# L1 of a two-layer perceiver: TensorE in source order, keys and values in turn, sums spread by one product

## The chip, the cores and the metric

The kernel runs on one core of a Trainium2 chip. The metric is the time of one execution on the device, in microseconds (us). Before the change three runs gave 3542.09, 3542.24 and 3546.8 us; their median is 3542.24.

The core has engines with a queue each: TensorE (PE: matmuls and transposes), VectorE (DVE), ScalarE (ACT), GpSimd (POOL), and SyncE (SP), which issues nearly all DMAs. They meet through semaphores: an instruction that waits for another engine's result stands at the head of its own engine's queue.

## The reference

A stream `x` of 16 batches x 64 tokens x 512 passes through two layers. Layer 0 (cross attention with a similarity, causal attention, a mixture of experts) isn't touched by the change. Layer 1, in the kernel's terms and shapes:

```
u   = layernorm(x)                                     # 1024 rows: 8 tiles of 128, two batches each
q   = u @ x1_Wq + bq                                   # 16 heads of 32
k   = ctx[b] @ x1_Wk + bk ; v = ctx[b] @ x1_Wv + bv    # 1601 context rows a batch
p   = softmax(mask(q k^T / sqrt(32)))                  # masked keys: no weight
x   = x + (p v) @ x1_Wo + bo                           # cross attention
x   = x + differential_attention_block(layernorm(x))   # within a token, 32 x 32 scores of 16 elements,
                                                       # then a 512-2048-512 ReLU layer
x   = x + ternary_ffn(layernorm(x))                    # 8-bit activations, ternary weights, a
                                                       # 3-tap depthwise convolution, SiLU
```

All is float32 on PE but the ternary products, which are bfloat16.

## The kernel before, in words

`l1_layer` (from L674) walks over steps: one step is one batch `b` and one block `f` of four heads (128 of 512 columns), so 16 x 4 = 64 steps. Two batches share a tile of 128 rows.

A step needs the transposed keys `kT` of its block, 1601 columns in four chunks (`KC`: 384, 384, 384, 449), and the values `v` of the half that its heads lie in (13 blocks of 128 keys, 256 columns). They come from the transposed context, `ctxT`, which is loaded in the same four chunks (`load_ctx`, L751).

- `project_k` (L760) computes one chunk of one block: 4 matmuls into a bank of the pool `ps_mm` (four banks), and ACT moves it out with its bias (L767).
- `project_v` (L770) computes the blocks of one chunk: 4 matmuls of 256 columns into a bank each, and one ACT copy each (L782).
- `scores` (L818) takes two chunks, for the two pairs of heads: four banks, four matmuls over 64 rows (`qbd` holds the queries, block by block), and DVE copies what the mask leaves into the rows `p` (L832), which GpSimd has filled with -1e15 (L1192).
- DVE takes the negated row maximum (L1202), and ACT the exponential with its sum (L1203). This is the softmax of the step; its sums go to `rs8`, 8 columns a batch.
- `transpose_keys` (L171) turns the `p` of the step before, 13 transposes for each of its two halves, into the two banks of `ps_tp`; ACT copies them out as `pT` (L185).
- `attend` (L836) multiplies `pT` with `v`: 52 matmuls of 64 columns by 32, into a bank of `ps_acc` (two banks) that lasts for the batch.
- `finish` (L851), once a batch: a transpose of `rs8`, a reciprocal on 8 partitions (L857), 8 matmuls with the constant `spread` that repeat each head's factor over 32 rows (L861), a copy, and a product with the attention. After an odd batch also the output projection and `residual` (L189: DVE, then GpSimd).

Three generators give work that runs beside the steps: `ternary_weights` during the first pair of batches, `later(t)` (the rest of the layer for tile `t`, from L915, ending in `last`, L1086) during the pair after the tile's own, and `queries` (L785) for the next tile. They stop at each `yield`, and `run` advances them by some stops. `later` has PE work (projections, the hidden layer, ternary products), much DVE work (`products`, L889: 24 pairs of a product L895 and a sum L896), norms (`ln_stats`, `ln_apply`, `norm_T`), and short chains through several engines (`across`, L1070; the transposes of `top` at L1149, of `o` at L992).

What the source names is not the order in which an engine works: a scheduler builds each engine's queue from priorities and modelled times. So the queue of PE before has, for instance, single key matmuls between groups of transposes. Banks of a pool are given out as they come free.

Of the kernel before, what the change touches and what calls it, by code (L numbers as in the profile page):

```python
# [10 lines left out]
F32 = mybir.dt.float32  # L11
# [3 lines left out]
AF = mybir.ActivationFunctionType  # L15
# [4 lines left out]
P = 128  # L20
# [653 lines left out]
def l1_layer(g, d, out):  # L674
# [5 lines left out]
    with ExitStack() as es:  # L680
# [5 lines left out]
        vpool = pool("x1_v", 15)  # L686
# [16 lines left out]
        spread = one.tile([NP, 2, NC, P], F32, tag="spread", name="spread")  # L703
        nc.gpsimd.memset(spread, 0.0)
        for j in range(2):
            for pl in range(2):
                nc.gpsimd.memset(spread[:, j, :, ds((2 * pl + j) * HDX, HDX)], 1.0)
            nc.gpsimd.affine_select(
                out=spread[:, j], in_=spread[:, j], compare_op=ALU.is_equal, fill=0.0,
                base=0, pattern=[[-2, NC], [-1, 2], [0, 2 * HDX]], channel_multiplier=1,  # L710
            )
# [39 lines left out]
        def load_ctx(b):  # L751
            for n, (k0, w) in enumerate(KC):
                tag = "ctxT" if n < 3 else "ctxT_last"
                t = cpool.tile([P, NC, w], F32, tag=tag, name=tag, bufs=None if n < 3 else 1)
                nc.sync.dma_start(
                    out=t, in_=g.ctx_T[b, :, k0 : k0 + w].rearrange("(c p) k -> p c k", p=P)
                )
                ctxs[b, n] = t

        def project_k(b, f, n):  # L760

            w = KC[n][1]
            ps = mm(g)
            mm_k(g, ps[:, :w], lambda c: wk[:, c, ts(f, P)], lambda c: ctxs[b, n][:, c, :])
            tag = "kT" if n < 3 else "kT_last"
            kT = kpool.tile([P, w], F32, tag=tag, name=tag, bufs=None if n < 3 else 2)
            nc.scalar.activation(kT, ps[:, :w], AF.Identity, bias=col(g, "x1_bk", f))  # L767
            kTs[b, f, n] = kT

        def project_v(b, half, n):  # L770

            k0, w = KC[n]
            for k in range((w + P - 1) // P):
                kw = min(P, w - k * P)
                ps = mm(g)
                mm_k(
                    g, ps[:kw, :256],
                    lambda c: ctxs[b, n][:, c, ds(k * P, kw)],
                    lambda c: wv[:, c, ts(half, 256)],
                )  # L780
                v = vpool.tile([P, 256], F32, tag="v", name="v")
                nc.scalar.copy(v[:kw], ps[:kw, :256])  # L782
                vs[b, half, k0 // P + k] = v[:kw]

        def queries(t):  # L785

            u = apool.tile([P, D], F32, tag="u2", name="u")
            ln_apply(g, u, g.x[t], ln_stats(g, small, [g.x[t]]), 0)
            yield
            uT = apool.tile([P, NC, P], F32, tag="u2T", name="uT")  # L790
            nc.scalar.copy(uT, transpose4(g, u))
            yield
            ps = mm(g).rearrange("p (f x) -> p f x", f=NC)
            for f in range(NC):
                if f % 2 == 0:
                    wq = load_cols(d["x1_Wq"], f // 2)
                mm_k(g, ps[:, f, :], lambda c: wq[:, c, ts(f % 2, P)], lambda c: uT[:, c, :])
            qT = spool.tile([P, NC, P], F32, tag="qT", name="qT", bufs=2)
            at, n = _COLS["x1_bq"]
            nc.vector.tensor_tensor(  # L800
                qT, ps, g.cols[:, at : at + n].unsqueeze(2).to_broadcast([P, NC, P]), ALU.add
            )
            qTs[t] = qT
# [47 lines left out]
        def finish(b, po, rs8):  # L851
            t, hb = divmod(b, 2)

            pt = mm(g, tag="tp")
            nc.tensor.transpose(pt[:NP, :P], rs8, g.ident)
            rsT = small.tile([NP, P], F32, tag="rsT", name="rsT")
            nc.vector.reciprocal(rsT, pt[:NP, :P])  # L857
            pr = mm(g, tag="tp")
            for f in range(NC):
                for j in range(2):  # L860
                    nc.tensor.matmul(  # L861
                        pr[:, ts(f, S)], lhsT=spread[:, j, f, :], rhs=rsT[:, ts(j, S)],
                        start=(j == 0), stop=(j == 1),
                    )
            rb = spool.tile([P, NC, S], F32, tag="rb", name="rb")
# [13 lines left out]
            )  # L879
            py = mm(g, tag="acc")  # L880
# [20 lines left out]
        def norm_T(src, gname, bname):  # L901

            z = apool.tile([P, D], F32, tag="z", name="z")
            ln_apply(g, z, src, ln_stats(g, small, [src]), 0)
            yield
# [9 lines left out]
        def later(t):  # L915
# [73 lines left out]

# [14 lines left out]
            for k in range(4):  # L1004
                ps = mm(g).rearrange("p (f x) -> p f x", f=4)
                hid = apool.tile([P, 4, P], F32, tag="hid", name="hid", bufs=2)
                for f in range(4):
                    if f % 2 == 0:
                        w = load_cols(d["W1T"][:, ts(k, 512)], f // 2)
                    mm_k(g, ps[:, f, :], lambda c: w[:, c, ts(f % 2, P)], lambda c: h2T[:, c, :])  # L1010
                    nc.scalar.activation(  # L1011
# [58 lines left out]
        def across(c):  # L1070

            dg = spool.tile([P, P], F32, tag="dg", name="dg")
            nc.vector.tensor_scalar(dg, g.ident, c, None, ALU.mult)
            pb = mm(g, tag="tp")
# [11 lines left out]
        def last(t):  # L1086
# [10 lines left out]
            nc.vector.tensor_scalar(inv, inv, g.tinv[:, 0:1], None, ALU.mult)  # L1097
            yield
# [5 lines left out]
            invb = across(inv)  # L1104
# [3 lines left out]
            for k in range(4):  # L1108
# [4 lines left out]
                yield  # L1113
# [33 lines left out]
            yield  # L1147
            pt = mm(g, tag="tp")
# [4 lines left out]
            nc.vector.tensor_scalar(inv, inv, g.tinv[:, 1:2], None, ALU.mult)  # L1153
            yield
            scb = across(sc)
            qT = apool.tile([P, NF, P], BF16, tag="att", name="qT")
            for k in range(4):
# [4 lines left out]
                if k % 2 == 1:  # L1162
                    yield
            po = mm(g, tag="acc")
# [11 lines left out]


        load_ctx(0)
        for n in range(len(KC)):
            project_k(0, 0, n)  # L1180
            project_v(0, 0, n)
        run(queries(0))
        pending = None
        behind, asked = ternary_weights(), iter(())
        for b in range(B):
            mk, qbd = prepare(b, qTs[b // 2])
            for f in range(NC):
                bk, fk = divmod(b * NC + f + 1, NC)
                ps_ = []
                for j in range(2):  # L1190
                    p = ppool.tile([P, S2], F32, tag="p", name="p")
                    nc.gpsimd.memset(p, -1e15)  # L1192
                    ps_.append(p)
                scores(b, f, (0, 1), ps_, mk, qbd)
                if pending is not None:
                    first = transpose_keys(g, ptpool, pending[2][0], (0, 1), nc.scalar.copy)
                scores(b, f, (2, 3), ps_, mk, qbd)
                if f == 0:
                    sums = small.tile([P, NP], F32, tag="rs8", name="rs8")
                for j, p in enumerate(ps_):  # L1200
                    negm = small.tile([P, 1], F32, tag="negm", name="negm")
                    nc.vector.tensor_reduce(negm, p, AX.X, ALU.max, negate=True)  # L1202
                    nc.scalar.activation(  # L1203
                        p, p, AF.Exp, bias=negm, accum_out=sums[:, 2 * f + j : 2 * f + j + 1]
                    )
                if pending is not None:
                    pTs = [
                        first + transpose_keys(g, ptpool, pending[2][0], (2, 3), nc.scalar.copy),
                        transpose_keys(g, ptpool, pending[2][1], None, nc.scalar.copy),
                    ]  # L1210
                before = pending
                if b % 2 == 1 and f == 0 and b + 1 < B:
                    asked = queries(b // 2 + 1)
                for n in range(len(KC)):
                    if bk < B:
                        project_k(bk, fk, n)
                    if n == 0:
                        if before is not None:
                            attend(*before[:2], pTs, before[3])
                            if f == 0:  # L1220
                                finish(b - 1, *before[3:])
                        if f == 0:
                            po = mm(g, tag="acc")
                            if b % 2 == 0 and b > 0:
                                behind = later(b // 2 - 1)
                        pending = (b, f, ps_, po, sums)
                    if f % 2 == 0 and b + f > 0:
                        project_v(b, f // 2, n)
                    run(behind, 1 if f % 2 == 1 or b % 2 + f == 0 and n < 2 else 3 + f // 2)
                    if n == 3:  # L1230
                        run(asked, 1)
                if f == 2 and b + 1 < B:
                    load_ctx(b + 1)
            if b % 2 == 1:
                run(behind)
        pTs = [transpose_keys(g, ptpool, p) for p in pending[2]]
        attend(*pending[:2], pTs, pending[3])
        finish(B - 1, *pending[3:])
        run(later(NT - 1))


# [121 lines left out]
```

## Time and profile before

| quantity | value |
|---|---|
| median of three runs | 3542.24 us |
| the profiled execution: its time | 3548.19 us |
| its span, first to last instruction | 3546.4 us |
| granted clock of TensorE, mean | 0.968 |
| first scores of L1 | 843.3 us |
| first scores of the last step | 3324.2 us |
| busy: PE, DVE, ACT, POOL | 3275.7, 1652.8, 1140.0, 377.5 us |
| `ps_mm` of values, 256 columns, full chunks | 2304 passes, 523.7 us |
| `ps_mm` of keys, 384 columns | 1536 passes, 555.2 us |
| scores, 384 columns (L824) | 768 passes, 197.7 us |
| transposes of `p` (L182), all layers | 1768 passes, 255.4 us |
| copies under the mask (L832) | 512, 270.4 us |
| row maxima (L1202) | 128, 226.5 us |
| exponentials (L1203) | 128, 208.0 us |

How to read it: a float32 matmul shows as two passes. Ends of matmuls are modelled, so a row's mean is longer than the distance from one start to the next. In the views of waits and of the timeline, a bracket gives the idle time of the engine just before, and whose result ended it; a row with "x8" merges eight neighbours.

### The profile page before, as it was taken

How to read it: one execution, taken by the hardware profiler on the slowest of the kernel's cores; microseconds unless marked ns; L12 is line 12 of the kernel's file. 1: busy time of each engine (PE TensorE's matmuls, PEld its weight loads, DVE VectorE, ACT ScalarE, POOL GpSimd, SP SyncE). 2: the span in 40 equal slices, each digit the busy share in tenths (PEclk: the TensorE clock that was granted, in tenths of full speed). 3: DMA queues.
4: the chain of work that ended last, by engine and by line, in shares of the span. 5: the costliest groups of instructions: out<-in, count | busy, mean ns of one | idle time of the engine just before them, and what ended most of it. 6: DMA issues, size and time to landing. Idle time of an engine off the chain costs nothing. (4 is left out here: it accounts for less than half of the span.)

```text
span 3546.4 us, 49781 instructions
## 1 busy us (share of the span) xinstructions
PE 3275.7 (92%) x21128; PEld 2194.3 (62%) x21128; DVE 1652.8 (47%) x2632; ACT 1140.0 (32%) x2220; POOL 377.5 (11%) x340
## 2 busy tenths in 40 slices
PE   6999999998999999999999999999999999999815
PEld 2444445685677666766767666667667676666514
DVE  2121223116525825653493458256534934581573
ACT  1111021112333434334333434343343334343402
POOL 0000003332101100010001001000100010010000
PEclk9999999999999999999999999999999999999957
DMA  9988413875611133113222321331132123213113
GB/s 361 313 288 304 140 36 107 283 254 174 196 50 50 40 107 103 57 43 123 95 65 74 111 75 40 107 103 57 44 124 97 61 74 111 75 41 107 63 36 122
DMA packets 267374, 418.03 MB, mean 118 GB/s; under 512 B 20736, under 2 KB 164224, under 8 KB 267152
## 3 DMA queue, kind: packets, MB, share of 16 engines
q1 hardware_dynamic: 254656, 370.28, 31.7%
q0 software_dynamic: 12496, 44.57, 3.6%
q8 instruction: 166, 2.72, 0.3%
q14 instruction: 56, 0.46, 0.0%
HBM read 392.26 MB, written 22.54 MB: 117 GB/s over the span
## 5 line engine op out<-in xcount | busy, mean ns | idle before, releaser
L146 PE MATMUL ps_mm<-ctxT,wkv 128*128 128x384 f32 x1536 | 555.2, 492 | 2.0 <-DVE p L832 0.4
L146 PE MATMUL ps_mm<-wkv,ctxT 128*128 128x256 f32 x2304 | 523.7, 380 | 0.0
L146 PEld LDWEIGHTS ps_mm<-wkv,ctxT 128*128 128x128 f32 x2304 | 434.0, 190 | 80.1
L832 DVE COPY_PREDICATED p<-mk,ps_mm 128x384 f32<-128x384 uint8 (+1 forms) x512 | 270.4, 596 | 332.8 <-PE ps_mm L824 332.7
L1192 POOL MEMSET p<- 128x1601 f32 x128 | 185.7, 1453 | 1822.9 <-PE ps_tp L182 1819.1
L146 PEld LDWEIGHTS ps_mm<-ctxT,wkv 128*128 128x128 f32 x1536 | 272.6, 191 | 134.0 <-DVE p L832 7.8
L185 ACT COPY pT<-ps_tp 128x512 f32<-128x512 f32 x504 | 230.7, 504 | 356.2 <-PE ps_tp L182 356.1
L782 ACT COPY v<-ps_mm 128x256 f32<-128x256 f32 (+1 forms) x416 | 152.4, 370 | 417.4 <-PE ps_mm L146 416.7
L182 PEld LDWEIGHTS ps_tp<-ident,p 128*128 128x128 f32 (+1 forms) x1768 | 199.9, 143 | 135.0 <-issue 56.7
L182 PE MATMUL ps_tp<-ident,p 128*128 128x128 f32 (+1 forms) x1768 | 255.4, 282 | 6.4 <-ACT pT L87 3.0
L1202 DVE TENSOR_REDUCE negm<-p 128x1 f32<-128x1601 f32 x128 | 226.5, 1810 | 1.2
L146 PE MATMUL ps_mm<-wkv,ctxT_last 128*128 128x256 f32 (+1 forms) x1024 | 226.2, 379 | 0.0
L895 DVE TENSOR_TENSOR prod<-qkv 128x1024 f32<-128x1024 f32 x128 | 156.5, 1223 | 138.4 <-ACT qkv L927 134.8
L1203 ACT ACTIVATE p<-p,negm 128x1601 f32<-128x1601 f32 x128 | 208.0, 1627 | 15.1 <-DVE negm L1202 14.6
L146 PEld LDWEIGHTS ps_mm<-wkv,ctxT_last 128*128 128x128 f32 (+1 forms) x1024 | 181.1, 177 | 48.6 <-issue 12.1
L146 PE MATMUL ps_mm<-ctxT_last,wkv 128*128 128x449 f32 x512 | 206.4, 540 | 0.0
L824 PE MATMUL ps_mm<-kT,qbd 64*128 64x384 f32 x768 | 197.7, 531 | 8.1 <-DVE qbd L813 8.0
L767 ACT ACTIVATE kT<-ps_mm,cols 128x384 f32<-128x384 f32 x192 | 109.3, 579 | 188.7 <-PE ps_mm L146 188.7
L146 PEld LDWEIGHTS ps_mm<-hT,w 128*128 128x128 f32 x1024 | 132.2, 194 | 56.2 <-ACT hid L1011 40.6
L896 DVE TENSOR_REDUCE att<-prod 128x64 f32<-128x1024 f32 x128 | 155.8, 1217 | 3.7
L146 PEld LDWEIGHTS ps_mm<-ctxT_last,wkv 128*128 128x128 f32 x512 | 95.6, 190 | 81.1 <-issue 73.5
L146 PE MATMUL ps_mm<-hT,w 128*128 128x128 f32 x1024 | 142.6, 283 | 2.4 <-ACT hid L1011 1.0
(291 smaller groups left out, 3872.3 us busy)
## 6 DMA issues: line engine op xcount, KB each, us to landing
ctxT<-in_ctx_T_dram SPq DMA_DIRECT2D x48, 1024.0 KB, 10.4
ck<-in_ctx_dram SPq DMA_DIRECT2D x48, 1024.0 KB, 7.3
ctxT<-in_ctx_T_dram SPq DMA_DIRECT2D x48, 768.0 KB, 4.4
w<-in_W1T_dram SPq DMA_DIRECT2D x64, 512.0 KB, 4.6
w<-in_W2T_dram SPq DMA_DIRECT2D x64, 512.0 KB, 3.7
wt<-tern SPq DMA_DIRECT2D x64, 512.0 KB, 4.2
ctxT_last<-in_ctx_T_dram SPq DMA_DIRECT2D x16, 898.0 KB, 4.8
w<-in_x_Wq_dram SPq DMA_DIRECT2D x16, 512.0 KB, 3.8
```

What stands on the lines that cost most here:

```text
L146: g.nc.tensor.matmul(out, lhsT=lhs(c), rhs=rhs(c), start=(c == 0), stop=(c == n - 1))
L182: g.nc.tensor.transpose(pt[:kw, j, :], p[:, k0 + j * P : k0 + j * P + kw], g.ident)
L185: (out_of or (lambda o, i: evac(g, o, i)))(pT[:kw, :blocks, :], pt[:kw, :blocks, :])
L767: nc.scalar.activation(kT, ps[:, :w], AF.Identity, bias=col(g, "x1_bk", f))
L782: nc.scalar.copy(v[:kw], ps[:kw, :256])
L824: nc.tensor.matmul(bank[:, : KC[n][1]], lhsT=qbd[ts(j, 2 * HDX), f].rearrange("p j s -> p (j s)"), rhs=kTs[b, f, n][ts(j, 2 * HDX), :], st ...
L832: nc.vector.copy_predicated(ps_[j][:, k0 : k0 + w], mk[:, k0 : k0 + w], bank[:, :w])
L895: nc.vector.tensor_tensor(pr, qv.unsqueeze(2).to_broadcast([P, CH, 32, 16]), kv, ALU.mult)
L896: nc.vector.tensor_reduce(out[:, ts(i, CH * 32)], pr.rearrange("p i j d -> p (i j) d"), AX.X, ALU.add)
L1192: nc.gpsimd.memset(p, -1e15)
L1202: nc.vector.tensor_reduce(negm, p, AX.X, ALU.max, negate=True)
L1203: nc.scalar.activation(p, p, AF.Exp, bias=negm, accum_out=sums[:, 2 * f + j : 2 * f + j + 1])
```

## The change

- PE's queue is no longer scheduled: `tc.manual_schedule` around all of L1 puts PE's instructions in the order of the source. The other engines are scheduled as before.
- The loop over steps becomes a function `step` that names its work in a fixed order: first scores, transposes, a unit of projection, transposes, a stop of `later` (`slot`), and so on.
- Before, each step computed the keys for the next step, and even steps also half the values. Now odd steps compute keys, of two blocks at once (`project_k(b, h)`), and even steps values (`project_v(b, half)`).
- Values are computed two blocks to a bank, with one copy for both; the pool of values has 10 tiles of two blocks in place of 15 of one.
- `spread` and the transpose of `rs8` go. `widen` builds on DVE, from the reciprocals and a constant `side`, a matrix with each head's factor in its 32 columns, and one matmul a block with `fold` (two identities of 64, one above the other) gives the factors.
- Chains get more stops, so that a transpose comes one stop later than what it needs (two `yield` before it); `across` is cut in two (`diagonal` on DVE, then the matmul); the four ReLUs follow all 16 matmuls of their block; the stop between a ternary product and its scaling goes.

```diff
-        def project_k(b, f, n):
...
+        def project_k(b, h):
+
+            for n, (_, w) in enumerate(KC):
+                for f in (2 * h, 2 * h + 1):
+                    ps = mm(g)
+                    mm_k(g, ps[:, :w], lambda c: wk[:, c, ts(f, P)], lambda c: ctxs[b, n][:, c, :])
...
+                    yield
+        def project_v(b, half):
+
+            for k in range(0, len(KT), 2):
+                ps = mm(g).rearrange("p (j n) -> p j n", j=2)
+                v = vpool.tile([P, 2, 256], F32, tag="v", name="v")
...
+                nc.scalar.copy(v[:kw, : len(blocks)], ps[:kw, : len(blocks)])
+                yield
+        def widen(rs8):
...
+            nc.vector.reciprocal(r8, rs8)
+            wide = spool.tile([P, NP, 2, HDX], F32, tag="wide", name="wide")
+            nc.vector.tensor_tensor(
+                wide, r8.unsqueeze(2).unsqueeze(3).to_broadcast([P, NP, 2, HDX]),
+                side.unsqueeze(1).unsqueeze(3).to_broadcast([P, NP, 2, HDX]), ALU.mult,
+            )
-        def finish(b, po, rs8):
+        def finish(b, po, wide):
...
-            pt = mm(g, tag="tp")
-            nc.tensor.transpose(pt[:NP, :P], rs8, g.ident)
-            rsT = small.tile([NP, P], F32, tag="rsT", name="rsT")
-            nc.vector.reciprocal(rsT, pt[:NP, :P])
             pr = mm(g, tag="tp")
             for f in range(NC):
-                for j in range(2):
-                    nc.tensor.matmul(
-                        pr[:, ts(f, S)], lhsT=spread[:, j, f, :], rhs=rsT[:, ts(j, S)],
-                        start=(j == 0), stop=(j == 1),
-                    )
+                nc.tensor.matmul(
+                    pr[:, ts(f, S)],
+                    lhsT=wide[:, ts(f, 2)].rearrange("p h j d -> p (h j d)"), rhs=fold,
+                    start=True, stop=True,
+                )
...
+        def step(b, f, before, mk, qbd):
...
+            def slot():
+                if resting == 0:
+                    run(behind, 1)
+            resting = b % 2 + f == 0
...
+            if f % 2 == 0:
+                work = project_v(b, f // 2) if b + f > 0 else iter(())
+            else:
+                bk, h = (b, 1) if f == 1 else (b + 1, 0)
+                work = project_k(bk, h) if bk < B else iter(())
+            unit = 2 - f % 2
+            scores(b, f, (0, 1), ps_, mk, qbd)
+            if f == 0 and before is not None:
+                wide = widen(sums[b - 1])
+            turn(0, (0, 1))
+            run(work, unit)
+            turn(0, (2, 3))
+            slot()
+            turn(1, (0,))
+            scores(b, f, (2, 3), ps_, mk, qbd)
+            for j, p in enumerate(ps_):
+                negm = small.tile([P, 1], F32, tag="negm", name="negm")
+                nc.vector.tensor_reduce(negm, p, AX.X, ALU.max, negate=True)
+                nc.scalar.activation(
+                    p, p, AF.Exp, bias=negm, accum_out=sums[b][:, 2 * f + j : 2 * f + j + 1]
+                )
+            turn(1, (1,))
+            run(work, unit)
+            turn(1, (2, 3))
+            slot()
+            run(work, unit)
+            ending = iter(())
+            if before is not None:
+                attend(*before[:2], pTs, pos[before[0]])
+                if f == 0:
+                    ending = finish(b - 1, pos.pop(b - 1), wide)
+                    run(ending, 1)
+            slot()
+            run(work, unit)
+            run(ending)
...
+            resting = 0
+            run(asked, 1)
+            slot()
+            for _ in range(5 - f % 2):
+                run(work, 1)
+                slot()
+            run(asked, 1)
+            run(work)
+            slot()
+            if f == 2 and b + 1 < B:
+                for n in range(len(KC)):
+                    load_ctx(b + 1, n)
...
-        load_ctx(0)
-        for n in range(len(KC)):
-            project_k(0, 0, n)
-            project_v(0, 0, n)
-        run(queries(0))
...
+        with tc.manual_schedule(engines={mybir.EngineType.PE}):
+            for n in range(len(KC)):
+                load_ctx(0, n)
+            run(project_k(0, 0))
+            run(project_v(0, 0))
+            run(queries(0))
```

Here `turn(j, ns)` transposes chunks `ns` of half `j` of the step before.

## Prediction

> **What bounds the kernel now.** I read the busy shares first, then the granted clock, then one stretch of the second layer (which I call L1), then who waits for whom there, and last single steps.
>
> ```profile
> PE 3275.7 (92%) x21128; PEld 2194.3 (62%) x21128; DVE 1652.8 (47%) x2632; ACT 1140.0 (32%) x2220; POOL 377.5 (11%) x340
> ...
> PE   6999999998999999999999999999999999999815
> ...
> PEclk9999999999999999999999999999999999999957
> ```
>
> TensorE (PE) is the bound from the tenth slice to the 37th. L1 repeats with a period of two batches, because one tile of 128 rows holds two: the even batch's first scores start at 1078.1, 1403.7, 1728.2, 2053.0, 2379.1, 2702.4 and 3028.5 us in the timeline, on average 325.1 apart. I name the eight steps of such a pair e0 to e3 and o0 to o3 (even or odd batch, f = 0 to 3). The windows view of one pair (busy us and count of PE, PEld, DVE, ACT and POOL, then clock and DMA):
>
> ```profile
> 2379.00:2702.40 323.40, 312.76 (x2252) 222.66 (x2251) 175.19 (x260) 129.18 (x252) 29.52 (x22) 1.00 0.26 82
> ```
>
> PE stands still for 10.6 of 323 us here. The waits of PE over the six pairs from 1078 to 3028 us say for whom:
>
> ```profile
> PE ps_acc L842 <- ACT pT L185: 24.2, 36, 1.3
> PE ps_mm L824 <- DVE p L832: 21.7, 23, 2.0
> PE ps_tp L1149 <- ACT pT L185: 7.4, 6, 1.2
> PE ps_mm L146 <- ACT oT L992: 4.0, 6, 0.7
> PE ps_mm L146 <- ACT uT L1103: 2.7, 6, 0.4
> ```
>
> They sum to 60.0 us, 10.0 a pair. A matmul's modelled end runs about 0.16 us past the next start (14 key passes of 0.323 are 4.52 us, shown as 4.68), so 77 waits hide another 2 us a pair: 12.0. That is all that a better order of PE can win; the rest is matmuls that stay.
>
> **The change part by part.**
>
> *Matmuls.* Keys, values, scores, attention and the later layers issue the same passes (a float32 matmul has two), so their sum stays; two value blocks in a bank only halve ACT's copies, which lie beside PE. *Sums:* now 16 passes take 1.93 us (963.50 to 965.43) plus a transpose of 0.11. Four matmuls in place of eight halve the passes: 0.96. Gain 1.07 a batch, 2.1 a pair; the new `wide` on DVE (one 512-wide operation, 0.69 like L877, plus a small reciprocal, against a reciprocal of 0.95) is issued some 12 us before it is used.
>
> *Waits removed:* at most the 12.0. Together 14.1 a pair.
>
> *Waits added.* In the built program PE follows the source, so nothing can be slipped in front of a late instruction, and everything behind it waits too. [...] If later matmuls could pass, the list below would be nothing and L1 would gain 14 a pair; by the rule each wait counts in full. The trace sides with the rule: the last L1149 idles PE 5.20 us at 3337 with an attend queued behind. I therefore follow chains through ACT's and DVE's built order.
>
> (1) *Step o3, the transpose of `top`.* In the built order ACT does, after the second score group, two copies, table load, exp, key copy, exp and only then the two `pT` copies; `top` needs the bank of the first. The same chain today, o3 at 2678, on PE and then on ACT:
>
> ```profile
> 2682.40 0.77 PE L182 MATMUL ps_tp<-ident,p 128*128 128x128 f32 x5
> ...
> 2685.86 4.68 PE L146 MATMUL ps_mm<-ctxT,wkv 128*128 128x384 f32 x14
> 2691.77 0.33 PE L1149 MATMUL ps_tp<-ident,top 128*128 128x128 f32 x1 [1.23 <-ACT pT L185]
> ```
>
> ```profile
> 2686.62 1.28 ACT L1203 ACT_TABLE_LOAD   x1 [1.11 <-DVE negm L1202]
> 2687.91 1.63 ACT L1203 ACTIVATE p<-p,negm 128x1601 f32<-128x1601 f32 x1
> ...
> 2689.54 1.61 ACT L1203 ACTIVATE p<-p,negm 128x1601 f32<-128x1601 f32 x1
> ...
> 2691.15 0.72 ACT L185 COPY pT<-ps_tp 128x512 f32<-128x512 f32 x2
> ```
>
> From the end of the scores (2682.40) to `top` it takes 9.4 us, and PE covers all but 1.23. After the change only 4 transposes (0.44), one key chunk (8 passes, 2.58) and 5 transposes (0.55) stand there, 3.6 us, as PE's built order shows (a `Matmult` is two passes, a transpose one; K is a key chunk):
>
> ```
> scores x4 | ident,p x4 | K | ident,p x4, x1 | ident,top | K | attend | K | dg,ones ...
> ```
>
> The wait is 5.8.
>
> [...] The row says 1.28, and exp follows 0.01 later. [...] I take the row.
>
> (2) *Attend behind both exps.* Scores to attend, by rows: copies end 1.65 us after the scores (four in 2.13, starting 1.0 after the group's start), maximum 1.77, exp 1.63 and again 1.63 with gaps of 0.1, a value or key copy 0.55, `pT` copies 0.75: 8.3, and 1.28 more with a table load (waits of this kind, 0.67 us on average, are the first row of the list above). PE's cover in a value step is 0.44+3.45+0.55+3.45 = 7.9. So e0 waits 0.4, o0 about 1.5, o2 about 2.0 (DVE's convolution sits between). e2 and e3 come out at 1.9 each, DVE being late. Sum 7.7.
>
> (3) *DVE late in e1 to e3.* Attention products of the later layer are 2 x 1.255 us a unit. A copy behind them in DVE's order waits:
>
> ```profile
> 2781.27 1.22 DVE L895 TENSOR_TENSOR prod<-qkv 128x1024 f32<-128x1024 f32 x1
> 2782.53 1.22 DVE L896 TENSOR_REDUCE att<-prod 128x64 f32<-128x1024 f32 x1
> 2783.78 1.22 DVE L895 TENSOR_TENSOR prod<-qkv 128x1024 f32<-128x1024 f32 x1
> 2784.92 0.58 DVE L832 COPY_PREDICATED p<-mk,ps_mm 128x384 f32<-128x384 uint8 x1
> ```
>
> Today six units run at the end of e0. After the change one and a half do, and 22.5 fall into e1 to e3: 56.5 us, with copies and maxima (3 x 7.75) and the softmax and scaling (about 14) 94 us, against PE work of 89.5. In the built order two product units stand between the two score groups' copies, so the banks come late. From e1's start, in us: its first copies (0.5 each, a 1.25 reduction between) end at 4.5, two units at 9.5, the next copy at 10.1, where PE stands ready at 8.7: 1.4. Seven units then hold DVE until 35.3; e2 starts at 31.3, wants its bank at 33.7 and has it at 35.9: 2.25. Its second group finds DVE busy from 38.7 to 45.0, bank at 45.65 against 43.15: 2.5. e3 the same way 0.85 and 2.5. Sum 9.5.
>
> (4) *Third transpose bank.* The source now has 4+1 transposes, then 4 more into the first bank, with ACT's key or value copy (0.55) ahead of the bank's own (0.50): freed 1.3 after the chunk, wanted at 0.55. That is 0.75 in the six steps whose slot there holds no PE work (o1 and o2 have some): 4.5.
>
> (5) *Normalization.* In e0 the transpose of `z` stands three value blocks (5.2 us) behind the output projection; the chain (residual, GpSimd, two norms) took 6.8 in the tail (3361.28 to 3368.04) and has a second norm interleaved here: 8.5, a wait of 3.3. In o0 the hidden layer follows its transposes at once, with four ACT rows of 0.38 each: 1.3. Sum 4.6.
>
> Together 32.1 a pair. Hand-followed chains overstate: a late PE lets the others catch up. The ends are 0 (all covered) and 32.1; I take three quarters, 24, since (1), the largest single wait, rests on a measured chain. Net 24 - 14.1 = +10 a pair, seven pairs +70.
>
> *The front.* PE waits 4.0 for `u` at 823 and 8.0 for `qbd` at 835. Ten more us of keys cover the first; DVE's reductions, which delayed `qbd`, now come earlier. But the second step's transposes follow two score groups with nothing between: some 6 us for maximum, table and exp. Net -5. Pair 0 (no later layers): waits of kinds 2 and 4, some 16, and DVE's weight rounding, some 5, against 235 measured less 223 of work: +10. The tail keeps its DVE chain (73.6 us of PE idle for L988); the last step, without key work, orders `top` before the final transposes: +3.
>
> *DMAs.* Context chunks keep bytes and place (after f = 2), and the built SP order puts weights in between, as before: 4.4 us to land, needed 20 later: nothing. Uncovered, a chunk costs up to 4.4 a batch.
>
> Sum: the profiled run took 3548.2, its span 3546.4; +70 - 5 + 10 + 3 = +78 gives 3624 of span. The median of the runs is 3542.2, so **3620**.
>
> **The rivals.** *Half the waits* (16 a pair): +2 x 7 + 8 = +22, 3564. For it: many of the waits are differences near 1 us. Against: (1). *Faster:* the cover holds. It decides at new waits of 13 a pair; with only (1) and half of (4), 8, L1 gains 6 a pair: 3542 - 43 + 8 = 3507; with none 3542 - 99 + 8 = 3451. For it: copies of scores now have a key or value chunk between the groups, where today 8 transposes (1.0 us) meet four copies (2.1). Against: the order of the exps before the copies, in six of eight steps. *DVE as the bound:* all 32.1 and more, some 35 a pair: +21 x 7 + 8 = 3697; for it 94 against 89.5, against it DVE's 175 us in a pair of 323. *The change does nothing:* the built order moves as the source says, so this is only a draw of gains and losses.
>
> **How the numbers follow.** Likeliest case (3585 to 3685) 0.50, half the waits (3550 to 3585) 0.20, faster 0.20, a draw 0.04, DVE-bound 0.06. 0.2% (7 us) is about what a measurement tells from no change. Range 3500 to 3685: it leaves out the DVE case and the better half of the faster one. Faster 0.20, same 0.04, slower 0.76.
>
> **What would show it.** Right: waits of PE for `pT` at `top` near 6 us in each o3, waits for `p` copies in e1 to e3, a pair period near 335, PE's idle time up from 10 to some 25 a pair, fewer passes under the sums. Wrong: a period under 325, or `top` and attend without waits, which would mean that ACT's order or PE's cover isn't as I read it.

## The result, and the profile after

The changed kernel takes 3590.82 us (median of 4 runs, 3588.24 to 3591.26) where the kernel before takes 3542.16 in the same series: 1.0133 times as long, 95% interval 1.0115 to 1.0150. The prediction was 3620, slower. The profiled execution has 3591.18 us and a span of 3589.4, 43.0 more than before.

Busy shares and slices, from the page of the changed kernel:

```profile
PE 3219.8 (90%) x20976; PEld 2161.4 (60%) x20984; DVE 1627.0 (45%) x2649; ACT 1097.0 (31%) x2028; POOL 372.0 (10%) x336
...
PE   6999999998999899999999998999899999989815
...
PEclk9999999999999999999999999999999999999957
```

PE is busy for 56 us less and the kernel takes 43 us more. Several slices of L1 that stood at 9 now stand at 8.

The pairs of batches start at 1091.6, 1425.2, 1757.6, 2088.7, 2419.6, 2753.1 and 3085.4 us: six periods of 332.3 on average, against 325.05. One of them in the windows view of the changed kernel (columns as before):

```profile
2419.60:2753.10 333.50, 310.16 (x2235) 221.49 (x2235) 172.35 (x262) 123.80 (x228) 29.21 (x22) 0.98 0.25 80
```

PE stands still for 23.3 us where it was 10.6. For whom, the waits of PE over these six pairs tell (line waited at, releaser: us in total, times, longest):

```profile
PE ps_acc L847 <- ACT pT L185: 35.4, 24, 1.8
PE ps_mm L146 <- DVE p L837: 33.3, 30, 1.9
PE ps_tp L1170 <- ACT pT L185: 32.8, 6, 5.5
PE ps_tp L182 <- ACT pT L185: 21.9, 36, 0.6
PE ps_tp L126 <- DVE z L117: 13.1, 6, 2.2
PE ps_mm L146 <- ACT hT L924: 3.6, 6, 0.6
```

Together 140.1 us, 23.35 a pair (before 10.0). L847 is attend, L146 after `p` a key or value chunk that wants a bank of scores, L1170 `top`, L182 the keys' transposes, L126 `z`.

The largest single one, step o3 of the fifth pair, from the timelines of PE and then of ACT:

```profile
2718.21 0.81 PE L829 MATMUL ps_mm<-kT,qbd 64*128 64x384 f32 x4
2718.95 0.66 PE L182 MATMUL ps_tp<-ident,p 128*128 128x128 f32 x4
2719.45 2.75 PE L146 MATMUL ps_mm<-ctxT,wkv 128*128 128x384 f32 x8
...
2722.03 0.71 PE L182 MATMUL ps_tp<-ident,p 128*128 128x128 f32 x5
...
2728.20 0.47 PE L1170 MATMUL ps_tp<-ident,top 128*128 128x128 f32 x1 [5.46 <-ACT pT L185]
2728.47 5.33 PE L146 MATMUL ps_mm<-ctxT,wkv 128*128 128x384 f32 x8
```

```profile
2722.58 1.28 ACT L1248 ACT_TABLE_LOAD   x1 [2.35 <-DVE negm L1247]
2723.88 1.63 ACT L1248 ACTIVATE p<-p,negm 128x1601 f32<-128x1601 f32 x1
...
2725.51 1.61 ACT L1248 ACTIVATE p<-p,negm 128x1601 f32<-128x1601 f32 x1
...
2727.12 0.56 ACT L765 ACTIVATE kT<-ps_mm,cols 128x384 f32<-128x384 f32 x1
2727.58 0.73 ACT L185 COPY pT<-ps_tp 128x512 f32<-128x512 f32 x2
```

`top` has been ready long before; what it lacks is a bank of the transposes, and the copy that empties it stands on ACT behind a table load, two exps and a key copy. The key chunk behind `top` needs none of that and waits with it. Its eight passes then take 5.33 us, where the chunk ahead took 2.75: this comes back below.

### The profile page after: what moved, and what is told of

It reads as the page before. It is cut to its first block, busy times and chain, and to the rows that moved or that the text cites. A ratio compares the mean times of both kernels' runs of the same rounds, so it can differ in the third digit from the quotient of the medians.

```text
span 3589.4 us, 49320 instructions
## 1 busy us (share of the span) xinstructions
PE 3219.8 (90%) x20976; PEld 2161.4 (60%) x20984; DVE 1627.0 (45%) x2649; ACT 1097.0 (31%) x2028; POOL 372.0 (10%) x336
## 4 chain that ended last, share of the span: by engine, by line
PE 63%; DVE 24%; ACT 6%; DMA 4%; issue 2%; POOL 1%; SPq 1%; ACTq 0%; POOLq 0%; DVEq 0%
PE ps_mm L146 37%; PE ps_acc L146 7%; DVE prod L909 6%; DVE att L910 4%; DVE p L837 4%; PE ps_mm L829 3%; DVE negm L1247 3%; PE ps_acc L1034 3%; PE ps_tp L182 3%; PE ps_mm L240 2%; ACT p L1248 2%; PE ps_acc L847 2%; PE ps_acc L274 2%; DVE o L910 2%; DMA ck<-in_ctx_dram 2%
## 5 line engine op out<-in xcount | busy, mean ns | idle before, releaser
L146 PE MATMUL ps_mm<-ctxT,wkv 128*128 128x384 f32 x1536 | 538.4, 499 | 23.8 <-DVE p L837 23.8
L146 PE MATMUL ps_mm<-wkv,ctxT 128*128 128x256 f32 x2304 | 523.9, 381 | 18.9 <-DVE p L837 18.9
L146 PEld LDWEIGHTS ps_mm<-wkv,ctxT 128*128 128x128 f32 x2304 | 427.4, 190 | 76.3 <-DVE p L837 22.5
L146 PEld LDWEIGHTS ps_mm<-ctxT,wkv 128*128 128x128 f32 x1536 | 288.3, 195 | 209.5 <-DVE p L837 29.0
L182 PE MATMUL ps_tp<-ident,p 128*128 128x128 f32 (+1 forms) x1768 | 260.6, 280 | 39.2 <-ACT pT L185 30.3
L182 PEld LDWEIGHTS ps_tp<-ident,p 128*128 128x128 f32 (+1 forms) x1768 | 199.1, 141 | 157.1 <-issue 74.0
L146 PE MATMUL ps_mm<-wkv,ctxT_last 128*128 128x256 f32 (+1 forms) x1024 | 236.6, 386 | 0.0
L786 ACT COPY v<-ps_mm 128x512 f32<-128x512 f32 (+1 forms) x224 | 122.4, 549 | 314.8 <-PE ps_mm L146 314.0
L146 PEld LDWEIGHTS ps_mm<-wkv,ctxT_last 128*128 128x128 f32 (+1 forms) x1024 | 182.7, 180 | 37.5
L146 PE MATMUL ps_mm<-ctxT_last,wkv 128*128 128x449 f32 x512 | 199.4, 539 | 0.0
L829 PE MATMUL ps_mm<-kT,qbd 64*128 64x384 f32 x768 | 164.0, 509 | 4.1 <-DVE qbd L818 4.1
L146 PEld LDWEIGHTS ps_mm<-ctxT_last,wkv 128*128 128x128 f32 x512 | 97.1, 190 | 91.3 <-issue 82.0
L847 PE MATMUL ps_acc<-pT,v 128*32 128x64 f32 (+1 forms) x6656 | 106.5, 220 | 47.7 <-ACT pT L185 47.3
L847 PEld LDWEIGHTS ps_acc<-pT,v 128*32 128x32 f32 (+1 forms) x6656 | 96.2, 110 | 78.5 <-ACT pT L185 65.3
## 6 DMA issues: line engine op xcount, KB each, us to landing
ctxT<-in_ctx_T_dram SPq DMA_DIRECT2D x48, 1024.0 KB, 10.6
```

Of the source, the lines that this page charges most:

```text
L146: g.nc.tensor.matmul(out, lhsT=lhs(c), rhs=rhs(c), start=(c == 0), stop=(c == n - 1))
L182: g.nc.tensor.transpose(pt[:kw, j, :], p[:, k0 + j * P : k0 + j * P + kw], g.ident)
L786: nc.scalar.copy(v[:kw, : len(blocks)], ps[:kw, : len(blocks)])
L829: nc.tensor.matmul(bank[:, : KC[n][1]], lhsT=qbd[ts(j, 2 * HDX), f].rearrange("p j s -> p (j s)"), rhs=kTs[b, f, n][ts(j, 2 * HDX), :], st ...
L847: nc.tensor.matmul(po[ts(r, HDX), ts(f, S)], lhsT=vs[b, f // 2, k][:, ts(4 * (f % 2) + r, HDX)], rhs=pTs[r // 2][k][:, ts(r % 2, S)], star ...
```

## The experiments

All twelve runs (median; ratio to the kernel before with 95% interval; mean period of six pairs; waits of PE that the profile lists, a pair):

| kernel | us | ratio | pair | waits |
|---|---|---|---|---|
| before | 3542 to 3544 | 1 | 325.05 | 10.0 |
| changed | 3590.8 | 1.0133 [1.0115, 1.0150] | 332.3 | 23.35 |
| e_sched | 3486.8 | 0.9845 [0.9829, 0.9862] | 317.65 | 7.0 |
| e_bman | 3857.6 | 1.0890 [1.0871, 1.0908] | 365.5 | 37.9 |
| e_fold | 3526.8 | 0.9950 [0.9933, 0.9967] | 323.3 | 10.1 |
| e_exps | 3553.9 | 1.0031 [1.0021, 1.0042] | 327.7 | 17.2 |
| e_top | 3566.2 | 1.0062 [1.0045, 1.0079] | 328.1 | 21.0 |
| e_half | 3539.4 | 0.9989 [0.9982, 0.9996] | 329.8 | 19.5 |
| e_tpz | 3587.5 | 1.0129 [1.0112, 1.0146] | 331.5 | 19.85 |
| e_tp | 3554.0 | 1.0032 [1.0020, 1.0043] | 327.35 | 17.7 |
| e_four | 3504.0 | 0.9893 [0.9874, 0.9912] | 320.15 | 12.4 |
| e_five2 | 3502.1 | 0.9878 [0.9861, 0.9894] | 320.0 | 11.9 |
| e_mends | 3471.8 | 0.9795 [0.9779, 0.9812] | 315.8 | 9.2 |
| e_best1 | 3481.4 | 0.9828 [0.9802, 0.9855] | 318.5 | 6.8 |

### The three parts of the change, apart

**e_sched**: all but the order.

```
-        with tc.manual_schedule(engines={mybir.EngineType.PE}):
+        if True:
```

> The changed kernel with PE's order left to the planner again; the repacked keys and values, the new place of each piece and the sums by an identity stay. Theory (the order is what costs): PE's waits fall from 23 to near 12 us a pair, and with 2 us of sums saved the kernel comes out at or a little under the kernel before, 3520 to 3550. Rival (repacking costs): it stays near 3590.

3486.8: better than either theory, 56 us under the kernel before and 104 under the changed one. The repacking is no cost but a gain, and the order alone costs 14.65 us a pair net (the order also wins something, in the scores; that is counted below). Waits of PE over six pairs:

```profile
PE ps_mm L146 <- DVE p L837: 22.1, 12, 2.3
PE ps_acc L847 <- ACT pT L185: 14.9, 18, 1.6
PE ps_tp L126 <- DVE z L117: 2.7, 6, 0.5
PE ps_mm L829 <- ACT v L786: 1.2, 6, 0.2
PE ps_mm L146 <- ACT hT L924: 1.0, 6, 0.2
```

No line for `top` and none for the transposes' third bank (L182). The timeline of PE in o3 shows what the planner did, from the second transposes on:

```profile
2646.66 2.75 PE L146 MATMUL ps_mm<-ctxT,wkv 128*128 128x384 f32 x8
...
2649.24 0.71 PE L182 MATMUL ps_tp<-ident,p 128*128 128x128 f32 x5
...
2649.78 5.33 PE L146 MATMUL ps_mm<-ctxT,wkv 128*128 128x384 f32 x16
...
2654.95 0.27 PE L1170 MATMUL ps_tp<-ident,top 128*128 128x128 f32 x1
2655.15 1.66 PE L847 MATMUL ps_acc<-pT,v 65*32 65x64 f32 x104
```

ACT's order is as late as in the changed kernel, but two more key chunks (16 passes, 5.33 us at a granted clock of 1.00) are slipped in front of `top`, and it finds its bank free. That is what a fixed order takes away.

**e_bman**: the order alone. The L1 loop of the kernel before, unchanged, is put under the same line that fixes PE's order.

```
+        with tc.manual_schedule(engines={mybir.EngineType.PE}):
             load_ctx(0)
             for n in range(len(KC)):
                 project_k(0, 0, n)
...
```

> The kernel before with one part of the change alone: PE follows the order of its source, nothing else is touched. There the second scores follow four score matmuls and eight transposes, and attend follows all transposes and one key chunk. Theory (a fixed order turns short cover into waits): the second scores wait about 2 us and attend 4 to 5 us in each of eight steps, besides the chains of the later layers; a pair grows by 30 to 50 us and the kernel to 3780 to 3900. So the change's new places for the work earn most of that back. Rival (the order of PE costs little by itself, the repacking does): within 20 us of 3542.

3857.6, within the range: +40 a pair. So the new places of the work, with the repacking, earn back most of what the fixed order costs in the old ones (the sums are 1.8 of these 33 us a pair, see e_fold); the first line of its waits is attend's, 92.3 us in 36 waits of up to 3.8.

**e_fold**: the sums alone. `widen`, `fold` and the four matmuls of the changed `finish` are put into the kernel before.

```
-            pt = mm(g, tag="tp")
-            nc.tensor.transpose(pt[:NP, :P], rs8, g.ident)
...
-                for j in range(2):
-                    nc.tensor.matmul(
-                        pr[:, ts(f, S)], lhsT=spread[:, j, f, :], rhs=rsT[:, ts(j, S)],
...
+                nc.tensor.matmul(
+                    pr[:, ts(f, S)],
+                    lhsT=wide[:, ts(f, 2)].rearrange("p h j d -> p (h j d)"), rhs=fold,
```

> The kernel before with the sums by an identity alone: widen on DVE, four matmuls in place of a transpose and eight, nothing else. Theory: 1.07 us less PE work in each of 16 batches, 17 us: 3525. Rival (PE stands idle elsewhere by what is saved, or the planner moves other work for the worse): no change, 3540 to 3550.

Minus 16.8 us, 1.05 a batch. This term of the prediction (1.07) is settled.

### What PE waits for in the fixed order

**e_exps**: PE's order untouched, one exp later on ACT.

```
             scores(b, f, (2, 3), ps_, mk, qbd)
-            for j, p in enumerate(ps_):
-                negm = small.tile([P, 1], F32, tag="negm", name="negm")
-                nc.vector.tensor_reduce(negm, p, AX.X, ALU.max, negate=True)
-                nc.scalar.activation(
-                    p, p, AF.Exp, bias=negm, accum_out=sums[b][:, 2 * f + j : 2 * f + j + 1]
-                )
             turn(1, (1,))
             run(work, unit)
             turn(1, (2, 3))
+            for j, p in enumerate(ps_):
...
             slot()
```

> One edit to the changed kernel: a step's maxima and exps are named after the last transposes of the keys instead of ahead of them. PE's order is the same; on ACT the second exp then stands behind the last two pT copies, where it stood ahead of them. Theory (PE in a fixed order waits for pT copies that stand behind exps of 1.63 us on ACT): attend's waits, 5.9 us a pair, mostly vanish, top's 5.5 falls to about 3.9, a pair is shorter by 5 to 7.5, the kernel by 35 to 55 us: 3535 to 3555. Rival (the repacked keys and values, or DVE, set the pace, and ACT's order only decides where the wait is shown): the waits move to the copies of the scores and the time stays within 10 us of 3591.

3553.9, 37 us less than the changed kernel, within the theory's 35 to 55; a pair wins 4.6, a little less than the 5 to 7.5 expected. Of its waits:

```profile
PE ps_mm L146 <- DVE p L837: 33.0, 24, 3.1
PE ps_tp L1170 <- ACT pT L185: 23.1, 6, 3.9
...
PE ps_acc L847 <- ACT pT L185: 1.3, 6, 0.2
```

Attend's 35.4 us shrink to 1.3 and `top`'s 5.5 to 3.9: one exp (1.63) off the chain. Waits for copies of scores stay at 33, and a new kind appears, 7.5 us for copies of values (not shown).

**e_top**: one more place for `top`.

```
             yield
             yield
+            yield
             pt = mm(g, tag="tp")
             nc.tensor.transpose(pt[:, :P], top, g.ident)
```

> The changed kernel with the transpose of top named one place later: behind attend of step o3 instead of ahead of the key chunk before attend. Theory (both wait for the same pT copies, which come late on ACT): top's 5.5 us go, but attend, at 2.6 us of key chunk behind the transposes, now waits about 3.5, so a pair wins 2 and the kernel 14: 3570 to 3580. Rival (the place of top is the cause by itself): all 5.5 are won in seven pairs, 38 us: 3552.

3566.2: 25 us less, between the two. As the theory says, attend takes over (first line below, now with six more waits of 3.0); the listed waits fall by 2.4 a pair, but the period falls by 4.2, as PE's busy time falls by 1.8 too (308.9 to 307.1), though the matmuls are the same.

```profile
PE ps_acc L847 <- ACT pT L185: 53.7, 30, 3.0
PE ps_mm L146 <- DVE p L837: 33.4, 30, 1.9
```

The clock accounts for this: over the six pairs its records show 51.2 us at half rate in the changed kernel (granted clock 0.98 in three pairs, 0.99 in three) and 23.9 in e_top (0.99 in all six). Windows of o3 in the changed kernel: the chunk ahead of `top`, the one behind it, and the next (the third number from the end is the granted clock):

```profile
2719.50:2722.00 2.50, 2.50 (x10) 1.42 (x9) 2.50 (x5) 0.58 (x1) 0.00 (x0) 1.00 0.05 10
2728.50:2733.70 5.20, 5.20 (x9) 2.33 (x8) 1.23 (x7) 0.00 (x0) 0.00 (x0) 0.50 0.02 3
2735.40:2738.00 2.60, 2.60 (x16) 1.63 (x9) 0.00 (x0) 0.00 (x0) 0.00 (x0) 1.00 0.03 6
```

Behind these 5.46 us without work PE's granted clock is 0.50; eight passes take 5.33 us where the chunk ahead took 2.75. From the start of this chunk to the start of what follows, the half clock adds 1.5 to 2.6 us in each of the six pairs, 1.9 on average. So the wait at `top` costs 5.5 and about 1.9 on top of it.

**e_half**: half of the later layers' products on DVE are left out.

```
+            nc.gpsimd.memset(out, 0.0)
             for i in range(n // CH):
+                if i % 2 == 1:
+                    yield
+                    continue
```

> The changed kernel with every second unit of attention products of the later layers left out (zeros in their place); their slots stay empty. Theory (products on DVE hold up copies of scores in e1 to e3): waits for p copies, 5.6 us a pair, fall below 1, attend's in e2 and e3 fall with them, a pair goes from 332.3 to 324 to 327; outside the pairs the tail, where PE stands idle for these products, is shorter by about 30. Together 3505 to 3530. Rival (DVE has time enough and the fixed order of PE alone makes the waits): a pair stays within 2 of 332 and only the tail is shorter, 3555 to 3565.

Between the two: the tail is 30 us shorter as both said, but a pair only 2.5. Waits for `p` copies fall from 33.3 to 16.9, attend's only from 35.4 to 28.6: those of e2 and o0 are gone, but e3's rises from 1.7 to 2.9.

```profile
2172.18 5.28 PE L146 MATMUL ps_mm<-wkv,ctxT 128*128 128x256 f32 x16 [2.21 <-DVE p L837]
...
2220.92 1.66 PE L847 MATMUL ps_acc<-pT,v 65*32 65x64 f32 x104 [2.94 <-ACT pT L185]
```

DVE's load is a part of the loss, the smaller one. The first line also shows a wait of 2.21 and behind it 16 value passes in 5.28 us, where the 16 in the next place, at 2181.53, take 3.72.

**e_tpz** and **e_tp**: the third transpose bank, with `z` one place later and without.

```
-            turn(1, (0,))
             scores(b, f, (2, 3), ps_, mk, qbd)
...
-            turn(1, (1,))
+            turn(1, (0, 1))
```

and, in e_tpz alone, in `norm_T`:

```
             ln_apply(g, z, src, ln_stats(g, small, [src]), 0)
             yield
             yield
+            yield
             pt = transpose4(g, z)
```

> The changed kernel with two of the five pieces alone: the second keys' first transposes behind the second scores instead of ahead of them, and z's transpose one place later. Theory: the waits for the third transpose bank, 3.65 us a pair, go, but where attend waits after them (four of the six steps) it takes a part over; z's 2.2 falls to 0.5; a pair wins 3 to 4.5, the kernel 20 to 32: 3559 to 3571. Rival (attend's chain swallows all of the bank's waits): only z's 1.7 a pair are won, 12 us: 3579. Rival on the other side (waits add up freely): 5.3 a pair, 37 us: 3554.

> The changed kernel with the second keys' first transposes behind the second scores instead of ahead of them, and nothing else. Both moves of the run before together won 3 us; there z's later place also pushed each later piece by one, and a new wait of 4.1 us for pT copies stood at the first transposes of the ternary layers. Theory (the bank's wait is a real loss of its own where nothing late follows it in the step): e0 and e1 win 0.6 each, and in the steps that wait for exps the second scores start 0.44 earlier and the chain to attend with them: 2 to 3.5 a pair, 14 to 25 us: 3566 to 3577. Rival (the waits at attend and top take all of it over): within 7 us of 3590.

e_tpz misses: 3587.5, hardly anything won. e_tp, which was run to find out why, wins 37 us, more than either side expected. Waits of e_tp and then of e_tpz:

```profile
PE ps_acc L847 <- ACT pT L185: 44.8, 24, 4.3
PE ps_tp L1170 <- ACT pT L185: 30.2, 6, 5.0
PE ps_mm L146 <- DVE p L837: 14.7, 17, 1.9
```

```profile
PE ps_acc L847 <- ACT pT L185: 71.0, 30, 4.3
PE ps_tq L1123 <- ACT pT L185: 24.4, 6, 4.1
```

In both the line of L182 (21.9) is gone. In e_tp waits for copies of scores fall as well, from 33.3 to 14.7, which I hadn't counted; attend rises by 9.4, since in e1 the planner of ACT now puts a table load and both exps ahead of the last `pT` copy. The one `yield` more at `z` pushes every later piece by one place, and the first transposes of the ternary layers (L1123) come to stand where `top` stood: 4.1 us each, and attend 26.2 more than in e_tp. So a place that looks good for one piece cost 33 us through the pieces behind it.

### The same order, named better

**e_mends**: five pieces moved, PE still in the named order (the edits of e_exps, e_tp, e_top and `z` as shown, and the slots of the even batch):

```
             turn(0, (2, 3))
-            slot()
+            if b % 2 == 1:
+                slot()
...
             run(work)
             slot()
+            if b % 2 == 0:
+                slot()
```

> The changed kernel, still with PE in the named order, with five pieces named elsewhere: exps behind the last pT copies; the transposes of the second keys behind the second scores instead of one ahead of them; top one place later; the transpose of z one place later; in the even batch the later layers' first slot of a step at its end. Theory (the loss is where things are named, not that an order is fixed): the five kinds of wait fall from 23 to some 6 us a pair, a pair is near 316, the kernel 3465 to 3495, as with the planner's order. Rival (a fixed order can't follow the other engines, the waits move on): a pair stays above 325 and the kernel above 3540.

3471.8, 119 us less than the changed kernel and 72 less than before. Its waits (first two lines):

```profile
PE ps_mm L146 <- DVE p L837: 34.5, 17, 2.8
PE ps_acc L847 <- ACT pT L185: 8.3, 12, 1.0
```

What remains is DVE: 5.75 a pair for copies of scores, no less than in the changed kernel.

**e_four** takes the slots' move out again, **e_five2** puts the moved slot behind the maxima instead of at the step's end.

```
             turn(1, (2, 3))
...
             slot()
+            if b % 2 == 0:
+                slot()
```

> The five pieces less one: exps, the second keys' transposes, top and z as before, but the later layers' slots of the even batch where the change has them. Theory (products stand ahead of copies at the one end of a step or at the other, DVE is short of time in e1 to e3 either way): within 10 us of 3472. Rival (a slot between two score groups is what holds the copies up): the copies' waits rise again and the kernel to 3485 or more.

> The five pieces, with the even batch's first slot of a step moved only behind the maxima (two units in one place) instead of to the step's end. Theory (copies of the next step's first scores then meet a shorter row of products): waits for p copies fall from 5.75 to about 3 us a pair, a pair of 313, the kernel 3450 to 3462. Rival (the products of e1 to e3 fill DVE to the step's end anyway): within 5 us of 3472.

Both are 30 us slower than e_mends and like each other (3504.0, 3502.1). For e_four the rival's time holds but not its reason, since waits for copies of scores rise by only 4.4 us over six pairs; for e_five2 neither holds. Waits of e_four:

```profile
PE ps_mm L146 <- DVE p L837: 38.9, 21, 3.1
PE ps_tq L1123 <- ACT pT L185: 14.8, 6, 2.5
PE ps_acc L847 <- ACT pT L185: 13.3, 12, 1.6
```

In e_mends the slot at the end of e0 is one more than before (the first slot of e0 rests), so its later pieces stand one place earlier; in these two they don't, and the ternary transposes wait 2.5 in place of 0.6. I read the 30 us as the shift again, now undone; no run has the extra slot alone, so how much of it is DVE's order stays open.

**e_best1**: e_sched with e_exps' edit.

> The changed kernel with PE left to the planner and exps named behind the last pT copies. Theory: attend's remaining waits, 2.5 us a pair with the planner's order alone, go; a pair of 315 to 316, 3470 to 3482. Rival (PE then waits for the copies of the scores instead, DVE's products being in front of them): no change from the planner's order alone, 3487 within 5.

3481.4, which lies in the theory's range. But its runs spread from 3474 to 3494, so the 5 us to e_sched are not clear of noise. Attend's waits do go (14.9 to 1.6 us over six pairs), but new ones for the copies of scores and of values take their place, and the profiled pairs are no shorter (318.5, before 317.65): in mechanism the rival is nearer. The named order of e_mends is at 0.9795 and this at 0.9828; their intervals overlap. That of e_sched, 0.9845, does not overlap with e_mends: a well-named fixed order beat the planner's own by 15 us.

## Why the prediction was right, and where it wasn't

**Direction and mechanism.** PE follows the source, what is late holds up all behind it, and waits of PE rose by 13.35 us a pair. e_sched and e_bman show the order as the cause, e_exps that ACT's exps stand in the chain. Of the 78 us that the prediction added to the kernel, 49 came.

**The waits, term by term** (predicted, then measured a pair): (1) `top` 5.8, 5.5. (2) Attend 7.7, 5.9. (3) DVE late 9.5, 5.55. (4) The third bank 4.5, 3.65. (5) `z` and hidden layer 4.6, 2.8. Sum 32.1, measured 23.35; "I take three quarters, 24" was right, but the factor was set between 0 and 32.1 without a measurement: that it came out at 0.73 is in part luck. The largest error is (3): followed by hand, e2 alone was to lose 4.75 and lost 2.4 (0.90 and 1.49 in the fourth pair), I think because PE came later to each bank by the waits before it; no run shows that apart.

**The table load.** The row's 1.28 us held: after the change too the load takes 1.28, and exp follows 0.02 after its end (2722.58 to 2723.88). Between load and exp, where more would have lengthened the chain, nothing else shows.

**What a pair loses net: +10 predicted, +7.25 measured.** The step that failed is "issue the same passes, so their sum stays", and with it "12.0 a pair. That is all that a better order of PE can win; the rest is matmuls that stay". From 23.35 of waits to +7.25 something must have brought 16.1, not 14.1, although the half clock took some 2.9 of it back (1.9 behind `top`, 1.0 behind `z`): in all 19. The listed waits of before are 10.0 of this, and e_fold gives 1.8 to the sums. The largest part of the rest is in the scores: the same passes take less time. One group of second scores, in step e1, before and then in the changed kernel, each up to the row that follows it:

```profile
2441.30 1.10 PE L824 MATMUL ps_mm<-kT_last,qbd 64*128 64x449 f32 x3 [0.70 <-DVE p L832]
...
2443.53 0.66 PE L182 MATMUL ps_tp<-ident,p 128*128 128x128 f32 x4
```

```profile
2477.20 1.02 PE L829 MATMUL ps_mm<-kT_last,qbd 64*128 64x449 f32 x4
2478.06 0.81 PE L829 MATMUL ps_mm<-kT,qbd 64*128 64x384 f32 x4
2478.80 0.66 PE L182 MATMUL ps_tp<-ident,p 128*128 128x128 f32 x4
```

Eight passes take 2.23 us there and 1.60 here. A score matmul is 64*128 in its row, where a key pass is 128*128. In the changed kernel the eight passes start in four pairs, two neighbours 0.006 to 0.007 us apart; in the group of before the first and the last start alone, 0.46 and 0.43 from their neighbours, and the six between in pairs 0.02 to 0.04 apart. The changed kernel's second scores take 1.60 in all 48 steps of the six pairs, before 2.16 on average (half clock in five of six e3 is a part of that). Together both groups of a pair's eight steps fall from 31.7 us, 0.4 of them listed waits, to 26.1, which is 5.2 more than the lists show; some 2.0 are spread over other rows. This gain needs the fixed order and the new places: in the planner's order the same scores take 32.3 (e_sched), 33.4 (e_best1) and 31.8 (e_fold), in a fixed order with the old places 29.6 (e_bman), and 26.4 in e_mends, which is why e_mends can be faster than e_sched with more waits in its list. In e_sched the planner puts transposes between two score matmuls. Before, that banks come singly from DVE is my reading of the first row's wait; no run tests it. The prediction had 2.0 us for such hidden time.

**The last pair: the largest miss.** The spans' difference of 43.0 splits, by the starts of the pairs, into the front -0.8 (the first scores of L1 start at 842.5 us, before at 843.3; predicted -5), pair 0 +14.3 (+10), six pairs +43.4 (+60), and the last pair with the tail -13.9, where I had +13. "Seven pairs +70" counted the last like the others. But its o3 has no keys to compute, and after the change that is two blocks instead of one: a block is 24 passes of 0.323 and 8 of 0.377, 10.8 us, the same 10.8 that the front computes more and that I did count there. Nor does it have the wait of (1), as nothing of ACT stands in the chain late enough. A pair's +7.25 less 10.8, 5.5 and the 1.9 of half clock behind `top` is -10.9; the other 3 us stay open. PE in the last o3 of the changed kernel:

```profile
3376.59 1.10 PE L182 MATMUL ps_tp<-ident,p 128*128 128x128 f32 x8
3377.93 0.32 PE L182 MATMUL ps_tp<-ident,p 128*65 128x128 f32 x1 [0.24 <-ACT pT L185]
3378.41 0.33 PE L1170 MATMUL ps_tp<-ident,top 128*128 128x128 f32 x1 [0.17 <-ACT pT L185]
```

**The rivals.** Half the waits (16 a pair) was off: 23.35. "Faster" needed new waits under 13 a pair. DVE as the bound: e_half says no, since with half of the products gone a pair is only 2.5 shorter. "The change does nothing" is out too: the whole interval lies above 1.

## What to carry to other kernels

Fixing an engine's order is not good or bad in itself: with nearly the same matmuls it gave 3858, 3591 or 3472 us, by where the pieces were named (the first has the old sums and packing). Name a late result behind enough work that doesn't depend on it, and ask of each wait what stands in front of its releaser on the other engine; moving one exp there was worth as much as moving work on PE. After each move list all waits again, since one `yield` shifts every piece behind it. And compare distances from one start to the next, not only waits: 5 us a pair lay in rows that the profile counts as busy.

## What I had not expected of the hardware

Half clock after a wait. In the six pairs each of the six waits at `top` (5.46 to 5.47 us) is followed at once by four to eight key passes of 0.640 us instead of 0.323. Slower passes also follow some of the waits of 2.0 to 2.8 us in several kernels: 16 value passes take 5.28 us behind one of 2.21 in e_half (the line above) and 5.30 behind one of 2.46 in e_four, but 3.62 behind one of 2.46 in e_five2; eight key passes take 4.54 behind one of 2.75 in e_mends, but 2.85 behind one of 2.75 in e_four. It is not new with the change: before, the waits of 2.0 us for the second scores of e3 were followed by half clock in five of six pairs (transposes 0.213 us apart instead of 0.109), and in the changed kernel those of 2.2 us at `z` in four of six (value passes 0.427 apart instead of 0.216). The changed kernel's pairs have a granted clock of 0.98 to 0.99, those of before of 0.99 in five of six and 1.00 in the one without such a stretch, those of e_sched, whose longest wait is 2.3 us, of 1.00 in five of six and 0.99 in one. All six waits of 5.46 us were followed by half clock; of the waits of 2.18 us at `z` the one that ends at 1126.24 was, the one that ends at 1792.23 wasn't, so that the length of one wait alone doesn't decide. What else does, no run shows. The prediction left this out; it belongs to the price of term (1), 5.5 for the wait and about 1.9 for what follows.
